# A graph attention layer in blocks: X W stored by chunks and gathered in two parts, weights read from PSUM, one row turned earlier

## The chip, the cores and the metric

The kernel runs on one core of a Trainium2 chip. TensorE (PE) multiplies matrices, with its weight loads shown as PEld; VectorE (DVE), ScalarE (ACT) and GpSimd (POOL) work on elements; SyncE (SP) and POOL issue DMAs, and 16 DMA engines carry them between HBM and the on-chip memories SBUF and PSUM. The metric is the device time of one execution in microseconds. One execution was also taken by the profiler; the times in the texts that have two decimals are from its trace, and L1133 is line 1133 of the kernel before.

## The reference

Four layers, each x = layernorm(x + f(x)), over a graph of N = 2708 nodes with 128 features. `adj` is a dense 2708 x 2708 float32 matrix with mostly zeros.

```python
# layer 0: k = 4 nearest neighbours by distance of z, added to the adjacency
z = leaky_relu(lap_mul(A, x) @ W1 + b1, 0.1)
S = exp(-sqrt(d2(z) + 1e-10) / 2), kept for the 4 nearest of each row
out = lap_mul(S + A, x) @ W2 + b2
# layer 1: attention
XW = X @ W
s_col, s_row = XW @ a[:128], XW @ a[128:]
den = exp(leaky_relu(s_row[:, None] + s_col[None, :], 0.01))
num = A @ den
att = where(num != 0, den / num, 0)
H = A @ (att @ XW)
# layer 2: h = d A d x;  h @ W.T + b
# layer 3: relu([x, A x] @ W.T + b)
```

## The kernel before

**Tiles.** The nodes stand in 22 row tiles of 128 (FULL = 21 whole ones, and a last one of 20 nodes) and, as columns of `adjT`, in C = 6 chunks: four of 512, one of 384, one of 276. A pass over the adjacency takes, for each chunk, four panels of four row tiles each by DMA from SP (L175, 1 MB for a chunk of 512) into the slots of `ring`, and six resident row tiles (`res`).

**Layer 1 by ranks.** The term leaky_relu(s_row + s_col) takes one of two slopes, by whether s_row is over −s_col. So den is e^r e^c on one side of a threshold and e^.01r e^.01c on the other. The kernel sorts the columns of den by c into 44 blocks of 62 (two columns more carry running sums from block to block), and keeps for each node r, e^r (`e_r`), e^.01r (`f_r`) and, as a row on all partitions, e^.99r (`gb`). The stages:

- *Pass 2* of layer 0 (until about 443 us). `by_panels` runs the product; after each panel a list of chores with due times (`Due`, `at`) puts in work on the finished chunk: near gathers (L669, indirect DMAs from POOL that fetch the nearest neighbours' rows; DVE's near sums add them up), `norm0` (the layernorm), `turn` (transposes), `find_c`, `compare` (a mask of every node's c against one row tile's, on DVE), `times_w` (PE's X W, copied by ACT into `xwe`, which holds X W and r), `rank_rows` and `rank_columns` (ACT and PE count ranks).
- *The thresholds' wait* (443 to 463). The last chunk's chores; then rr (r copied out of `xwe`), e_r and f_r (L861 to L863), the store of X W to HBM from POOL (L874, and L877 for the last 20 rows), and the thresholds: `pick_c`, `to_all` (a product with ones that puts a sum on all partitions), and `lc`, the 32 columns of weights of each row tile.
- *The rank stage* (463 to 541). PE sums the adjacency over coarse blocks: `part_sum` (L1133) multiplies 128 x 32 of `lc` by a row tile of a chunk. Four row tiles stand in four groups of 32 columns of one PSUM tile, beside one another. `end_sums(c)` (ACT L1142, PE L1144, ACT L1145) folds them into `carry`. After every panel, `between(c, i0)` puts a chore into the order, which is written out by hand (`manual_schedule`) for PE, DVE and ACT:
  - `find_blocks`: each node's block; `into_places(js, ...)` (PE L981): the columns put in sorted places, as one-hot matrices times values;
  - `ranked`: `row_j` and `csort` out of `js`, a memset of `xws` (POOL L1002) and 22 gathers of the rows of X W in sorted order (POOL L1005); `g_col` = e^.99c and `g_inv` = e^−.99c;
  - `count`, `find_values` (DVE L1047 to L1054), `find_places`: the place of each node in its block's list; `into_places(sl, ...)` and `listed` (L1100 to L1109): the list of rows of each block, with e and f of each;
  - `on_all` (PE L871, ACT L872): a column of values, turned by 128 x 128 transposes into PSUM, then copied through Exp into a row on all partitions: `g_row` of csort at (2,0) to (2,12), and `gb` of rr at (3,20) and (4,0);
  - `weights`: the weights of each block's list, 62 columns each, made from `g_row` by DVE for odd blocks (L1117) and ACT for even blocks (L1121), and a maximum with 0 on DVE (L1124) for each four odd ones.
- *The block loop* (541 to 773). 44 steps, 22 pairs of blocks for each half of the columns. `load(i)` gathers the listed rows of the adjacency (POOL L1264, two a step) and two rows of `carry` (SP). `find_num` (PE L1384), `invert` (ACT Ln and Exp), DVE's mix, and `add` (PE L1243, with a block's 128 rows of `xws`, which ACT scales in place by `g_col` in the step's own turn). `load(i + 2)` is issued in step i. A power on POOL in the first steps (L254) gives `dinv`.
- Layers 2 and 3 (773 to the end).

PSUM tiles of the rank stage: three for `part_sum`, three of the kind `mis` for everything that is turned or put on all partitions, one each for the places and the counts. A dense version of layer 1 stands behind a branch (`flag`) and isn't run here.

Of the kernel before, what the change touches and what calls it, by code (L numbers as in the profile page):

```python
# [8 lines left out]
F32 = mybir.dt.float32  # L9
# [7 lines left out]
P = 128  # L17
# [35 lines left out]
def kernel(  # L53
# [96 lines left out]
    hT = big.tile([P, N], F32, tag="hT", name="hT")  # L150
# [99 lines left out]
    def inv_sqrt_of(dst, src, eps):  # L250

        if in_arm:
            nc.vector.tensor_scalar_add(dst, src, eps)  # L253
            nc.gpsimd.tensor_tensor(dst, dst, minus_half[:, : dst.shape[-1]], op=ALU.pow)  # L254
        else:
            nc.vector.tensor_scalar_add(dst, src, eps)
            inv_sqrt(dst, dst)
# [10 lines left out]
    def normalize(ts, xs):  # L268
# [7 lines left out]
        inv_sqrt_of(rstd[:, : t1 - t0], mv[:, t0:t1, 1], LN_EPS)  # L276
# [437 lines left out]
    def norm0(ts):  # L714
# [11 lines left out]
        normalize(ts, xs)  # L726
# [24 lines left out]
    def times_w(c, t):  # L751
# [3 lines left out]
        nc.scalar.copy(xwe[:p, t, : D + 1], po[:p, : D + 1])  # L755

# [33 lines left out]

    due = Due()
# [8 lines left out]
    def end_pass2(c, acc):  # L800
# [9 lines left out]
        if c < C - 1:  # L810
# [3 lines left out]
            for k, t in enumerate(ts):  # L814
                at(n + 13 + 2 * k, compare, t)
                at(n + 14 + 2 * k, times_w, c, t)
                if c == C - 2 and k == len(ts) - 1:
# [5 lines left out]
        else:  # L823
            for t in behind_last:
                at(n + 1, rank_rows, t)
            at(n + 2, norm0, ts)
            at(n + 3, turn, c)
            at(n + 4, find_c, c)
            for k, t in enumerate(ts):
                at(n + 5 + k, compare, t)  # L830
                at(n + 5 + k, times_w, c, t)
                at(n + 5 + k, rank_rows, t)
                at(n + 6 + k, rank_columns, t)

# [18 lines left out]

    with tc.tile_pool(name="rank", bufs=1) as rank:
# [6 lines left out]
        nc.vector.tensor_copy(rr, xwe[:, :, D])  # L861
        nc.scalar.activation(e_r, rr, AF.Exp)
        nc.scalar.activation(f_r, rr, AF.Exp, scale=0.01)  # L863

        def on_all(row, col, n0=0, n1=NQ):

            for o in range(n0 * P, min(n1 * P, row.shape[-1]), CW):
                e = min(row.shape[-1], o + CW)
                ps = mis_tile()
                for k in range(o, e, P):  # L870
                    nc.tensor.transpose(ps[:, k - o : k - o + P], col[:, k // P : k // P + 1].to_broadcast([P, P]), ident)  # L871
                nc.scalar.activation(row[:, o:e], ps[:, : e - o], AF.Exp, scale=0.99)  # L872

        nc.gpsimd.dma_start(  # L874
            xw_rows[: FULL * P, :].rearrange("(t p) d -> p t d", p=P), xwe[:, :FULL, :D]
        )
        nc.gpsimd.dma_start(xw_rows[FULL * P :, :], xwe[:LAST, FULL, :D])  # L877
# [11 lines left out]
        def pick_c(ranks, name):  # L889

            n = ranks.shape[-1]
            first = big.tile([P, n, T], F32, tag="hT", name=name)
# [15 lines left out]
        c_head = to_all(pick_c(edge[:, 0:NB:CH], "head"))  # L908
# [85 lines left out]
        hot_in = big.tile([P, N], F32, tag="hT", name="hot_in")  # L994
        hot = [ones_at(b_j, n) for n in range(3)]

        def ranked(js):
# [5 lines left out]

            for q in range(NQ):
                nc.gpsimd.indirect_dma_start(  # L1005
                    out=xws[:, q, :], out_offset=None, in_=xw_rows[:, :],
                    in_offset=bass.IndirectOffsetOnAxis(ap=row_j[:, q : q + 1], axis=0), bounds_check=N - 1,
                    oob_is_err=False,
                )
# [7 lines left out]
        two_b = wide.tile([P, T, NB], BF16, tag="wide", name="two_b")  # L1017
# [94 lines left out]
        def weights(lw, g_row, blocks):  # L1112
            for s in blocks:
                for b in (s, s + 1):
                    w, g = lw[:, b, 2:], g_row[:, b * (BJ + 2) + 2 : (b + 1) * (BJ + 2)]
                    if b % 2:
                        nc.vector.tensor_scalar(  # L1117
                            w, g, slot_e[:, b : b + 1], slot_f[:, b : b + 1], op0=ALU.mult, op1=ALU.add
                        )
                    else:  # L1120
# [456 lines left out]
```

## Time and profile before

| | us |
|---|---|
| four runs | 1117.26, 1115.72, 1133.07, 1126.06 |
| their median | 1121.66 |
| the profiled execution | 1112.36 |
| its span in the trace | 1110.5 |

| stage of the span | us | PE busy | DVE busy | ACT busy | POOL busy |
|---|---|---|---|---|---|
| load and pass 1, 0 to 157 | 157.0 | 124.41 | 97.72 | 13.10 | 12.49 |
| nearest neighbours, 157 to 284 | 127.0 | 126.30 | 122.50 | 73.09 | 9.08 |
| pass 2, 284 to 443 | 159.0 | 135.96 | 89.91 | 42.77 | 79.33 |
| thresholds' wait, 443 to 463 | 20.0 | 7.60 | 14.72 | 10.25 | 2.10 |
| rank stage, 463 to 541.2 | 78.2 | 64.50 | 35.19 | 20.67 | 32.94 |
| block loop, 541.2 to 773 | 231.8 | 222.57 | 213.47 | 157.00 | 94.83 |
| layers 2 and 3, 773 to 1110 | 337.0 | 322.49 | 72.10 | 27.55 | 27.08 |

The busy times are sums over the stretch named. In the lists of the trace, a line such as "507.19 4.95 PE acc L1133 x35" gives a start, a length, the engine, the tile written, the line of the kernel and the number of instructions. "issue" is time in which the engine waited for nothing that the profile shows. "another core or an unknown queue" and "remote" stand where the event that released an instruction has no writer in the trace. PEclk is the clock that TensorE was granted, as a share of the full one.

### The profile page before, as it was taken

How to read it: one execution, taken by the hardware profiler on the slowest of the kernel's cores; microseconds unless marked ns; L12 is line 12 of the kernel's file. 1: busy time of each engine (PE TensorE's matmuls, PEld its weight loads, DVE VectorE, ACT ScalarE, POOL GpSimd, SP SyncE). 2: the span in 40 equal slices, each digit the busy share in tenths (PEclk: the TensorE clock that was granted, in tenths of full speed). 3: DMA queues.
4: the chain of work that ended last, by engine and by line, in shares of the span. 5: the costliest groups of instructions: out<-in, count | busy, mean ns of one | idle time of the engine just before them, and what ended most of it. 6: DMA issues, size and time to landing. Idle time of an engine off the chain costs nothing.

```text
span 1110.5 us, 11430 instructions
## 1 busy us (share of the span) xinstructions
PE 1003.8 (90%) x3678; PEld 482.9 (43%) x3678; DVE 645.6 (58%) x1366; ACT 344.4 (31%) x626; POOL 257.9 (23%) x325
## 2 busy tenths in 40 slices
PE   0899999999978889597789999999999999999996
PEld 0356544444434456243233333333444644465444
DVE  5984549999824467863379999998212112122122
ACT  0000135555301235323557676666001100011000
POOL 4000000001575442035454343441111200000000
PEclk9989999999998899598999999999999999999998
DMA  9998330000474445595544444446574865574752
GB/s 341 369 303 274 114 113 1 1 0 1 145 253 149 136 139 186 194 346 160 152 114 140 137 128 145 154 144 207 165 254 152 269 227 190 175 248 141 254 156 76
DMA packets 109283, 190.30 MB, mean 171 GB/s; under 512 B 13570, under 2 KB 46610, under 8 KB 109214
## 3 DMA queue, kind: packets, MB, share of 16 engines
q1 hardware_dynamic: 91582, 151.86, 41.3%
q0 software_dynamic: 17632, 37.62, 11.0%
q8 instruction: 31, 0.51, 0.2%
q14 instruction: 38, 0.31, 0.1%
HBM read 214.37 MB, written 4.16 MB: 197 GB/s over the span
## 4 chain that ended last, share of the span: by engine, by line
PE 75%; DMA 8%; DVE 6%; issue 4%; POOL 3%; ACT 2%; another core or an unknown queue 2%; SPq 1%; POOLq 0%; DVEq 0%; ACTq 0%
PE acc L201 31%; PE acc L639 9%; PE num L1384 8%; PE hacc L1243 7%; PE acc L424 7%; DMA res<-in_adjT 3%; PE acc L629 2%; PE acc L1133 2%; DMA ring<-carry 2%; DMA ring<-in_adjT,slot_i 2%; PE mis L286 1%; DVE both L479 1%; DVE mask L767 1%; POOL ring L125 1%
## 5 line engine op out<-in xcount | busy, mean ns | idle before, releaser
L1264 POOL DMA_INDIRECT ring<-in_adjT,slot_i x88 | 96.1, 1092 | 136.3 <-PE num L1384 110.0
L1384 PE MATMUL num<-ring,lw 128*64 128x512 f32 (+1 forms) x528 | 118.1, 560 | 9.4 <-DMA ring<-in_adjT,slot_i 3.7
L1243 PE MATMUL hacc<-inv,xws 128*128 128x512 f32 (+1 forms) x264 | 111.6, 559 | 0.3 <-ACT inv L1221 0.3
L639 PE MATMUL acc<-zT,z 128*128 128x512 f32 (+4 forms) x264 | 106.9, 551 | 0.0
L1218 ACT ACTIVATE inv<-num,plain 128x1024 f32<-128x1024 f32 x88 | 80.6, 916 | 69.5 <-PE num L1384 64.2
L1228 DVE TENSOR_TENSOR err<-inv,num 128x1024 f32<-128x1024 f32 x88 | 74.8, 855 | 35.6 <-ACT inv L1221 34.3
L254 POOL TENSOR_TENSOR rstd<-rstd,minus_half 128x4 f32<-128x4 f32 (+1 forms) x18 | 17.3, 961 | 313.5 <-DVE rstd L253 313.5
L640 ACT COPY key<-acc 128x512 f32<-128x512 f32 (+3 forms) x132 | 70.2, 535 | 58.1 <-issue 29.8
L235 ACT COPY gb<-acc 128x512 f32<-128x512 f32 (+2 forms) x18 | 9.6, 535 | 251.1 <-PE acc L201 251.1
L669 POOL DMA_INDIRECT got<-y_rows,where x66 | 70.2, 1064 | 57.7 <-DVE near_sum L682 31.5
L201 PE MATMUL acc<-ring,y 128*128 128x512 f32 (+2 forms) x192 | 82.0, 556 | 1.4 <-DMA ring<-in_adjT 0.8
L1243 PEld LDWEIGHTS hacc<-inv,xws 128*128 128x128 f32 x264 | 46.5, 189 | 77.6 <-issue 43.6
L201 PE MATMUL acc<-ring,xs 128*128 128x512 f32 (+2 forms) x192 | 77.8, 549 | 0.0
L1235 DVE SCALAR_TENSOR_TENSOR inv<-gb,g_inv,inv 128x1024 f32<-128x1024 f32 x88 | 77.0, 914 | 0.1
L201 PE MATMUL acc<-ring,carry 128*128 128x512 f32 (+2 forms) x192 | 74.5, 542 | 0.0
L201 PE MATMUL acc<-ring,m_rows 128*128 128x512 f32 (+2 forms) x192 | 74.3, 542 | 0.0
L1232 DVE SCALAR_TENSOR_TENSOR inv<-err,inv 128x1024 f32<-128x1024 f32 x88 | 72.6, 864 | 0.1
L639 PEld LDWEIGHTS acc<-zT,z 128*128 128x128 f32 (+1 forms) x264 | 46.9, 186 | 53.9 <-issue 48.5
L1384 PEld LDWEIGHTS num<-ring,lw 128*64 128x64 f32 x528 | 38.2, 138 | 70.9 <-issue 48.9
L1221 ACT ACTIVATE inv<-inv 128x1024 f32<-128x1024 f32 x88 | 67.6, 768 | 2.8
L641 DVE MAX8 near<-key 128x8 f32<-128x2708 f32 (+1 forms) x22 | 65.3, 2970 | 3.5 <-ACT key L640 3.5
L642 DVE FIND_INDEX8 where<-near,key 128x8 uint32<-128x2708 f32 (+1 forms) x22 | 65.4, 2972 | 0.0
(323 smaller groups left out, 1322.3 us busy)
## 6 DMA issues: line engine op xcount, KB each, us to landing
ring<-in_adjT SPq DMA_DIRECT2D x86, 1024.0 KB
ring<-in_adjT SPq DMA_DIRECT2D x19, 768.0 KB
part<-in_adjT SPq DMA_DIRECT2D x12, 1024.0 KB
ring<-in_adjT SPq DMA_DIRECT2D x19, 552.0 KB
res<-in_adjT SPq DMA_DIRECT2D x4, 1280.0 KB
more<-in_adjT SPq DMA_DIRECT2D x4, 1024.0 KB
part<-in_adjT SPq DMA_DIRECT2D x3, 768.0 KB
part<-in_adjT SPq DMA_DIRECT2D x3, 552.0 KB
```

The lines of the kernel that those rows point to most:

```text
L201: nc.tensor.matmul(accs[c][: lhsT.shape[-1], :w], lhsT=lhsT, rhs=src, start=start, stop=stop)
L424: nc.tensor.matmul(accs[c][:, : cw[c]], lhsT=y[:, i, :], rhs=src[:, : cw[c]], start=first, stop=last)
L639: nc.tensor.matmul(pks[c][:p, : cw[c]], lhsT=z2[:, :p], rhs=zT[:, cs], start=False, stop=True)
L640: nc.scalar.copy(key[:p, cs], pks[c][:p, : cw[c]])
L669: nc.gpsimd.indirect_dma_start(out=got[:p, :], out_offset=None, in_=y2_rows[:, :], in_offset=bass.IndirectOffsetOnAxis(ap=where[:p, t, k : ...
L1218: nc.scalar.activation(inv, num[:, :w], AF.Ln, scale=plain[:, 0:1], bias=plain[:, 1:2])
L1228: nc.vector.tensor_mul(err, inv, num[:, :w])
L1232: nc.vector.scalar_tensor_tensor(inv, err, 2.0, inv, op0=ALU.subtract, op1=ALU.mult)
L1235: nc.vector.scalar_tensor_tensor(inv, gb[:, col : col + w], g_inv[:, q : q + 1], inv, op0=ALU.max, op1=ALU.mult)
L1243: nc.tensor.matmul(haccs[:, o:e], lhsT=xws[:, q, :], rhs=inv[:, o:e], start=(q == 0), stop=(q == NQ - 1))
L1264: nc.gpsimd.indirect_dma_start(out=rows[i][:KC, n, :], out_offset=None, in_=adj_half[:, :], in_offset=bass.IndirectOffsetOnAxis(ap=slot_i[ ...
L1384: nc.tensor.matmul(num[n * (BJ + 2) : (n + 1) * (BJ + 2), o:e], lhsT=lw[:, 2 * q + n, :], rhs=rows[i][:, n, c0 + o : c0 + e], start=True, ...
```

## The change

- *X W is stored chunk by chunk.* `keep_xw(c)` is put behind the last `times_w` of each chunk, so that its DMA issues stand in POOL's queue among the near gathers of pass 2. For the last chunk the three `times_w` come before the compares.
- *The last chunk's layernorm* takes its inverse square root by a power on POOL instead of ACT's square root and DVE's reciprocal, and ACT's Exp table is loaded before that chunk's transposes are copied.
- *gb in the thresholds' wait.* rr is copied before the last compare, `exp_r` adds `gb_col` = e^.99r, and the 22 transposes with their six ACT copies stand around the product that puts the head's sum on all partitions: eight before it, 14 behind. The row goes where `xwe` stood, so it waits for the last store of X W.
- *Weights from PSUM.* `g_row` is gone. `g_col` is turned by fours into a PSUM tile, and DVE and ACT read that tile, eight blocks to a tile, with a maximum after each.
- *Row tile 20* of the six chunks is summed for three chunks at once, each in a group of its own, as the last row tile of 20 nodes was before.
- *The chores of the rank stage* are put in another order: `find_blocks` at (0,8) instead of (0,20), three of the four parts of `js` and `find_values` at (1,4), `count` at (2,0), the fourth part, `find_places` and `ranked` at (2,4), the parts of `sl` at (3,0) and (3,4), weights from (3,8) to (4,8).
- *The X W gathers:* 14 (SOON) in `ranked` as before, eight in steps 0 to 7 of the block loop, each behind `load(i + 2)` on POOL.
- `m_rows` and `two_b` move to other buffers.

```diff
+    def keep_xw(c):
+        ts = chunk_tiles[c]
+        t0, t1 = ts[0], min(ts[-1] + 1, FULL)
+        nc.gpsimd.dma_start(
+            xw_rows[t0 * P : t1 * P, :].rearrange("(t p) d -> p t d", p=P), xwe[:, t0:t1, :D]
+        )
+        if t1 <= ts[-1]:
+            nc.gpsimd.dma_start(xw_rows[FULL * P :, :], xwe[:LAST, FULL, :D])
...
+    def find_r():
+        nc.vector.tensor_copy(rr, xwe[:, :, D])
+
+    def exp_r():
+        nc.scalar.activation(e_r, rr, AF.Exp)
+        nc.scalar.activation(f_r, rr, AF.Exp, scale=0.01)
+        nc.scalar.activation(gb_col, rr, AF.Exp, scale=0.99)
...
             for k, t in enumerate(ts):
                 at(n + 13 + 2 * k, compare, t)
                 at(n + 14 + 2 * k, times_w, c, t)
+                if k == len(ts) - 1:
+                    at(n + 14 + 2 * k, keep_xw, c)
...
-            at(n + 2, norm0, ts)
+            at(n + 1, exp_table)
+            at(n + 2, norm0, ts, True)
             at(n + 3, turn, c)
             at(n + 4, find_c, c)
+            for t in ts:
+                at(n + 4, times_w, c, t)
+            at(n + 4, keep_xw, c)
             for k, t in enumerate(ts):
+                if k == len(ts) - 1:
+                    at(n + 5 + k, find_r)
                 at(n + 5 + k, compare, t)
-                at(n + 5 + k, times_w, c, t)
...
-        nc.gpsimd.dma_start(
-            xw_rows[: FULL * P, :].rearrange("(t p) d -> p t d", p=P), xwe[:, :FULL, :D]
-        )
-        nc.gpsimd.dma_start(xw_rows[FULL * P :, :], xwe[:LAST, FULL, :D])
...
+        def turned(col, n0):
+
+            ps = mis_tile()
+            for k in range(n0, min(n0 + 4, NQ)):
+                nc.tensor.transpose(ps[:, (k - n0) * P : (k - n0 + 1) * P], col[:, k : k + 1].to_broadcast([P, P]), ident)
+            return ps
...
+            for n in range(n0, n1, 4):
+                ps, e = turned(col, n), min(row.shape[-1] - n * P, CW)
+                nc.scalar.copy(row[:, n * P : n * P + e], ps[:, :e])
...
-        c_head = to_all(pick_c(edge[:, 0:NB:CH], "head"))
+        head = pick_c(edge[:, 0:NB:CH], "head")
+        gb = wide.tile([P, T * D], F32, tag="wide", name="gb")[:, :N]
+        on_all(gb, gb_col, 0, 8)
+        c_head = to_all(head)
+        on_all(gb, gb_col, 8, T)
...
-            for q in range(NQ):
-                nc.gpsimd.indirect_dma_start(
...
+            for q in range(SOON):
+                fetch_xw(xws, q)
...
+        def weights(lw, n0):
+
+            g_all = turned(g_col, n0)
+            n1 = min(n0 + 4, NQ)
+            for b in range(2 * n0, 2 * n1):
+                o = (b - 2 * n0) * (BJ + 2) + 2
+                w, g = lw[:, b, 2:], g_all[:, o : o + BJ]
+                if b % 2:
+                    nc.vector.tensor_scalar(
+                        w, g, slot_e[:, b : b + 1], slot_f[:, b : b + 1], op0=ALU.mult, op1=ALU.add
+                    )
+                else:
+                    nc.scalar.activation(w, g, AF.Relu, scale=slot_e[:, b : b + 1], bias=slot_f[:, b : b + 1])
+            half = lw[:, 2 * n0 + 1 : 2 * n1 : 2, 2:]
+            nc.vector.tensor_scalar_max(half, half, 0.0)
...
-            if (c, i0) == (0, 20):
...
+            if (c, i0) == (0, 8):
+                c_edge = to_all(c_part)
+                find_blocks(c_edge)
...
+            if (c, i0) == (1, 4):
+                for n in range(3):
+                    into_places(work["js"], hot[n], val_q[:, :, :2, :], n)
                 hot.append(ones_at(b_j, 3))
+                find_values()
             if (c, i0) == (2, 0):
+                work["counts"] = count()
+            if (c, i0) == (2, 4):
                 into_places(work["js"], hot[3], val_q[:, :, :2, :], 3)
+                find_places(*work["counts"])
                 work["xws"] = ranked(work["js"])
...
+            if (c, i0) == (3, 0):
                 work["sl"] = js_pool.tile([P, CW], F32, tag="places", name="sl")
+                for n in range(3):
+                    into_places(work["sl"], hot[n], val_b, n)
                 hot.append(ones_at(pos, 3))
+            if (c, i0) == (3, 4):
                 into_places(work["sl"], hot[3], val_b, 3)
                 work["lw"] = listed(work["sl"])
...
+            if (c, i0) in ((3, 8), (3, 12), (3, 16), (4, 0), (4, 4), (4, 8)):
+                weights(work["lw"], 4 * work["groups"])
+                work["groups"] += 1
...
+                if i0 + 4 >= FULL - 1 and begins:
+                    for n in range(c, c + GROUPS):
+                        part_sum(n, FULL - 1, n - c, res[:, FULL - 1 - S, cols[n]])
...
+                late_q = list(range(SOON, NQ))
                 find_num(0, "wide")
                 find_inv(0, "wide")
                 for i, (h, q) in enumerate(steps):
                     if i + 2 < len(steps):
                         load(i + 2)
+                    if late_q:
+                        fetch_xw(xws, late_q.pop(0))
```

## The prediction

> **What bounds the kernel now.** I read the page's shares and its chain of waits first. TensorE carries three quarters of what ends last:
>
> ```profile
> PE 1003.8 (90%) x3678; PEld 482.9 (43%) x3678; DVE 645.6 (58%) x1366; ACT 344.4 (31%) x626; POOL 257.9 (23%) x325
> ...
> PE 75%; DMA 8%; DVE 6%; issue 4%; POOL 3%; ACT 2%; another core or an unknown queue 2%; SPq 1%; POOLq 0%; DVEq 0%; ACTq 0%
> ```
>
> So an edit pays only where PE stands idle. The change works between 355 and 590 us; busy time by stretches of the rank stage (columns: window; length; busy and instructions of PE, PEld, DVE, ACT, POOL; clock; DMA share; GB/s):
>
> ```profile
> 473.80:487.60 13.80, 13.80 (x99) 7.13 (x100) 5.36 (x11) 2.15 (x4) 0.00 (x0) 1.00 1.05 387
> 487.60:499.80 12.20, 10.89 (x86) 4.89 (x85) 11.67 (x21) 3.59 (x8) 10.20 (x7) 1.00 0.84 290
> 499.80:511.05 11.25, 11.25 (x89) 6.88 (x88) 1.61 (x7) 1.17 (x2) 8.68 (x9) 1.00 0.57 185
> 511.05:523.00 11.95, 4.94 (x12) 1.20 (x11) 6.56 (x29) 7.36 (x22) 7.81 (x8) 0.72 0.37 113
> 523.00:541.23 18.23, 13.95 (x109) 6.30 (x110) 0.33 (x2) 5.74 (x12) 6.26 (x6) 0.87 0.63 183
> ```
>
> PE is full until 511 and then loses 7.0 of 11.95 us, and 4.3 of the next 18.2. DMA is at 0.37 there, so panels aren't short. The chain of waits over that stretch (start, length, what):
>
> ```profile
> 507.19 4.95 PE acc L1133 x35
> ...
> 512.79 0.83 issue
> ...
> 516.20 1.72 issue
> ...
> 519.71 1.75 issue
> ...
> 522.91 2.18 PE mis L871 x9
> ...
> 533.39 3.37 another core or an unknown queue
> ...
> 537.26 2.03 another core or an unknown queue
> ...
> 541.23 3.14 PE num L1384 x8
> ```
>
> PE waits on nothing that is shown; single instructions come late. What else runs then, from the timelines of POOL, VectorE and ScalarE:
>
> ```profile
> 487.63 2.45 POOL L1002 MEMSET xws<- 128x2816 f32 x1 [29.00 <-PE js L981]
> 490.36 1.09 POOL L1005 DMA_INDIRECT xws<-xw_rows,row_j  x1 [0.28 <-DVE plain L1050]
> ...
> 519.99 1.00 POOL L1005 DMA_INDIRECT xws<-xw_rows,row_j  x1 [0.30 <-issue]
> 510.06 0.31 DVE L1100 TENSOR_SCALAR slot_i<-sl 128x44 uint32<-128x44 f32 x2 [8.40 <-PE acc L1133]
> 521.48 0.29 DVE L1124 TENSOR_SCALAR lw<-lw 128x248 f32<-128x248 f32 x1 [3.07 <-remote]
> 511.05 7.36 ACT L1121 ACTIVATE lw<-g_row,slot_f,slot_e 128x62 f32<-128x62 f32 x22 [3.24 <-issue]
> ```
>
> The 22 gathers of X W leave POOL every 1.31 us from 490.36 on. The list's matmuls (L981) end at 507.19, and DVE reads them at 510.06, 2.87 late; DVE then waits 3.07 for its own result. All this ends 2 us after the last gather. I read it as signals that arrive late under a long run of indirect DMAs; pass 2 shows it too (11.11 in the chain at 330.33, in a run of near gathers begun at 307; 6.21 at 357.88), and the burst of 372 to 388 has none. The lag began 10 to 21 us into a burst.
>
> The Trainium skill ("SBUF — State Buffer", "Who interferes with whom") lets only VectorE and GpSimd contend for a port, and TensorE and ScalarE never. The memset row agrees (VectorE's 2.11 us f_out beside its 2.45), the late PE row doesn't fit; by that rule shortening the burst would return nothing to PE.
>
> **The change, part by part** (on the clock of before's profile)
>
> *Pass 2.* Seven issues of the X W store stand among the near gathers, 0.60 to 1.50 us each (L877, L874). By the ends of the xwe copies (365.3, 394.0, 410.1, 431.8, 442.7, 450.4) and the bursts (372.2–387.8, 395.1–410.9, 416.8–424.3), most fall where POOL is idle; the second adds 0.6, the third holds tile 19's gathers from 408.3 to about 411.4, and those have some 6 us in hand. Zero; if not covered, up to 3. Behind a store that waits stand near gathers, and behind those DVE's near sums; the last store stands behind the power. Power on POOL costs 0.85 to 1.04 (L254) in place of 0.21 on ScalarE and 0.18 on DVE, on the way to the last chunk's xs, and rr's copy adds 0.18 before the last compare: **+0.6**. The table load (1.28, L862) moves into ScalarE's idle time of 446: zero, as DVE set the pace of the wait it leaves; 1.3 if it delays xT's copy.
>
> *Thresholds' wait.* 22 transposes (0.27 to 0.47) and six copies (0.60) of gb go where PE is busy 1.29 of 5.45 us, but three PSUM tiles and a clock of 0.50 make PE end them at about 464.6; part sums begin there, not at 462.95: **+1.6**, that +0.6 included. ScalarE's first gb copy also waits for the last X W store, whose buffer it takes; the old store's packets ran from 457 to 462.5 for 21 tiles, the last of the new ones has two and a bit, issued near 452: zero, or up to 5 us for PE, c_head and all of DVE's cuts behind it if that landing is late. Where gb's transposes stood (L871, 519.3 to 528.7) PE gets back 4.5, and row tile 20 summed for three chunks at once makes two passes of about 0.59 out of six of 0.4 to 0.6: about 2 more.
>
> *The list.* Between js (487.6) and the counts (493.72) DVE did 5.9 us of values (L1047 to L1054, memset's contention included); they now come while PE is at part sums. The list stands at 511.05 − 5.9 − 2.87 + 1.6 = **503.9**.
>
> *Weights.* Six copies of g_row (0.60) go. But both engines read one PSUM tile and each instruction waits for the other's: ScalarE 0.42 + VectorE 0.31 + two hand-offs of 0.04 is 0.81 a pair, 22 pairs **18 us**, where the 7.36 row of ScalarE ran beside VectorE. The bounds are 7.4 (no alternation) and 18; I take 18, as the built order has the waits. Behind a weight that waits are queued DVE's maxima, ScalarE's copies of end_sums and, on PE, the next transposes with all sums behind them, since there are three such PSUM tiles and end_sums needs one: 503.9 + 18 = 521.9, with two end_sums among them (2.2) 524.1, then the last three panels and two end_sums (5.3): the block loop starts at **529.4** if no signal is late, not at 541.23: **−11.8**. By TensorE's sum, 464.6 + 64.6 busy − 4.5 − 2 + 1.1 and 1.3 idle + 2.6 tail = 527.7, so weights bind by little.
>
> The skill's "PSUM — Partial Sum Buffer", "PSUM bank collisions raise a hardware error", says that two engines may not be at one bank together, reads included; it would make the alternation unavoidable and speaks against this change. No row of before has such a pair.
>
> *Late signals.* Fourteen gathers run from 494.1 to 512.4. With a lag from an age of 10 to 21 us, it covers 0 to 8 us of the weights, at 0.59 lost per us (7.0 of 11.95): 0 to 4.7; I take 2. The ring's gathers before the loop stay (3.37 + 2.03): 0 to 5.4; I take half, 2.7, as bursts with and without lag stand side by side. Start **534.1**, −7.1.
>
> *The loop.* Eight X W gathers join two ring gathers of 1.05 + 0.30 in steps of 4.9 us: 4.05 of 4.9, it fits; the product that reads a gathered row stands 14 steps later, so its landing costs nothing. The dinv power shows already what a POOL hold does:
>
> ```profile
> 558.18 2.92 POOL dinv L254
> ...
> 565.17 9.60 DMA ring<-in_adjT,slot_i
> ```
>
> It cost PE one wait of 3.14 us (574.82); a gather or two ahead of it adds 0 to 2.7. I take **+1.5**. Lags are the second rival.
>
> Sum: −7.1 + 1.5 = −5.6. The profiled execution took 1112.36 (span 1110.5), 9.3 below the median of the runs; I give the same difference to the median: 1121.66 − 5.6 = **1116**.
>
> **Rivals.** (1) No late signal any more: −11.8, and 0 to −3 more if the loop's wait goes: 1107 to 1110. For it: 14 gathers are a burst shorter than the 22 whose lag was seen from an age of 20 us; against it: near bursts lagged from 10. (2) Slower: eight loop steps keep POOL issuing at 83% of a burst's rate for 39 us, and signals between PE, ScalarE and VectorE run late there, where each step is a chain of hand-offs. With lag from 10 us on, 29 us × 0.59 = 17, net +10 or 1132; from the start 23, net +16 or 1138; it passes 1% once the lag begins within 8 us. Against: at two gathers per step, before's loop lags are at most 1.9 us. (3) The list is earlier, but each of the 44 alternations takes a lag of 0.15 us (6.6 us) and the ring's 5.4 stay: 529.4 + 12.0 = 541.4, with the loop's 1.5 1123. (4) The change doesn't do what it says: near gathers wait behind stores and pass 2 grows by 3 to 6, giving 1119 to 1122.
>
> **How the numbers follow.** About 1% (11 us) is what can be told from no change here, as the four runs spread over 17. Forecast (1112 to 1120) 0.38, rival 1 0.27, rival 2 0.18, rivals 3 and 4 0.17. Faster by over 1% (below 1110.4): rival 1 and a little of the forecast, 0.32. Slower (above 1132.9): rival 2 and a little, 0.20. Same 0.48. The range goes from 1104 (rival 1 with the loop's wait gone, and 1.7 more if weights run side by side and TensorE's 527.7 binds: 1105, less 1 for the rows' own spread) to 1132 (rival 2's milder end).
>
> **What would show it.** slot_e's writes (L1106 before) at about 504; ScalarE's and VectorE's weights in turn, 0.8 us a pair, 22 pairs; no single late PE instructions between 511 and 523; first num at 529 to 537; steps 0 to 7 at 4.9 us, with three gathers each. Wrong if the loop's first eight steps take more than 45 us, if weights run side by side, or if pass 2 ends over 2 us later.

## The result and the profile after

| | before | after |
|---|---|---|
| median of the runs, us | 1119.65 (69 runs) | 1121.47 (43 runs) |
| ratio to before, with its 95% interval | | 1.0018 (1.0004 to 1.0032) |
| profiled execution, us | 1112.36 | 1120.05 |
| its span | 1110.5 | 1118.3 |

The forecast was 1116, faster by 5.6 us; the measured change is a loss of 1.8 us, with 0.4 to 3.6 by the interval. The page of after, its busy shares and its chain of waits:

```profile
PE 1009.6 (90%) x3678; PEld 483.8 (43%) x3678; DVE 646.3 (58%) x1365; ACT 342.1 (31%) x620; POOL 265.4 (24%) x331
...
PE 60%; issue 17%; POOL 9%; DMA 7%; DVE 4%; ACT 2%; SPq 1%; POOLq 0%; another core or an unknown queue 0%; DVEq 0%; ACTq 0%
```

POOL stands in the chain with 9% where it had 3%, "issue" with 17% where it had 4%. A second trace of the same kernel (after_again, below) has 3% and 4% again, so these shares belong to one execution and nothing is read from them. The stretches of the rank stage, with the columns and the windows shown of before:

```profile
473.80:487.60 13.80, 13.71 (x92) 6.38 (x93) 8.94 (x20) 1.85 (x5) 0.00 (x0) 0.88 0.91 326
487.60:499.80 12.20, 12.20 (x104) 7.07 (x103) 6.53 (x13) 2.05 (x5) 6.10 (x4) 1.00 1.05 386
499.80:511.05 11.25, 10.44 (x77) 4.57 (x76) 2.95 (x11) 1.61 (x4) 8.59 (x9) 1.00 0.87 280
511.05:523.00 11.95, 5.14 (x9) 0.99 (x10) 3.22 (x10) 3.58 (x9) 2.45 (x3) 0.55 0.39 112
523.00:541.23 18.23, 12.75 (x90) 4.70 (x90) 4.41 (x14) 6.37 (x16) 7.33 (x7) 0.78 0.39 105
```

The hole is where it was: from 511 to 523 PE is busy 5.14 of 11.95 us (4.94 before). The timeline of ScalarE there:

```profile
508.87 0.40 ACT L1163 ACTIVATE lw<-mis,slot_f,slot_e 128x62 f32<-128x62 f32 x1 [0.41 <-issue]
509.68 0.40 ACT L1163 ACTIVATE lw<-mis,slot_f,slot_e 128x62 f32<-128x62 f32 x1 [0.41 <-issue]
515.80 0.40 ACT L1163 ACTIVATE lw<-mis,slot_f,slot_e 128x62 f32<-128x62 f32 x1 [5.71 <-remote]
516.61 0.40 ACT L1163 ACTIVATE lw<-mis,slot_f,slot_e 128x62 f32<-128x62 f32 x1 [0.41 <-DVE lw L1159]
```

The weights start 4 us earlier than before and go 0.81 us a pair, as worked out. Then ScalarE stands idle for 5.71 us where it waited 0.41 from pair to pair. (A hand-off is one engine's instruction waiting for another engine's.) This one came over 5 us late. POOL's last up-front gather, from its timeline:

```profile
513.11 1.00 POOL L890 DMA_INDIRECT xws<-xw_rows,row_j  x1 [0.30 <-issue]
```

It ends at 514.1, 1.7 us before ScalarE goes on. Two other stretches differ. Pass 1, which the change doesn't touch, waits longer for its last chunk; PE's row of before, then of after:

```profile
90.12 2.13 PE L424 MATMUL acc<-part,y 128*128 128x276 f32 x8 [1.27 <-DMA part<-in_adjT]
```

```profile
93.01 3.53 PE L427 MATMUL acc<-part,y 128*128 128x276 f32 x8 [3.52 <-DMA part<-in_adjT]
```

And in the block loop PE waits longer for rows of carry and for gathered rows (us in all, times, longest; 3.3 and 3.7 in all before):

```profile
PE num L1420 <- DMA ring<-carry: 5.8, 6, 1.6
PE num L1420 <- DMA ring<-in_adjT,slot_i: 5.3, 6, 1.8
```

### The profile page after: what moved, and what is told of

Read it like the earlier page. It is cut to its first block, busy times and chain, and to the rows that moved or that the text cites. A ratio compares the mean times of both kernels' runs of the same rounds, so it can differ in the third digit from the quotient of the medians.

```text
span 1118.3 us, 11444 instructions
## 1 busy us (share of the span) xinstructions
PE 1009.6 (90%) x3678; PEld 483.8 (43%) x3678; DVE 646.3 (58%) x1365; ACT 342.1 (31%) x620; POOL 265.4 (24%) x331
## 4 chain that ended last, share of the span: by engine, by line
PE 60%; issue 17%; POOL 9%; DMA 7%; DVE 4%; ACT 2%; SPq 1%; POOLq 0%; another core or an unknown queue 0%; DVEq 0%; ACTq 0%
PE acc L204 34%; PE acc L642 8%; PE acc L427 7%; POOL ring L1298 5%; DMA res<-in_adjT 3%; DMA ring<-in_adjT,slot_i 2%; PE acc L632 2%; POOL xws L890 1%; PE num L1420 1%; PE hacc L1277 1%; PE mis L289 1%; DMA part<-in_adjT 1%; DMA ring<-in_adjT 1%; ACT junk L792 1%; DVE both L482 1%
## 5 line engine op out<-in xcount | busy, mean ns | idle before, releaser
L1420 PE MATMUL num<-ring,lw 128*64 128x512 f32 (+1 forms) x528 | 121.7, 557 | 13.6 <-DMA ring<-carry 5.8
L643 ACT COPY key<-acc 128x512 f32<-128x512 f32 (+3 forms) x132 | 70.1, 534 | 58.2 <-issue 29.8
L204 PE MATMUL acc<-ring,y 128*128 128x512 f32 (+2 forms) x192 | 80.6, 548 | 1.3 <-DMA ring<-in_adjT 0.8
L645 DVE FIND_INDEX8 where<-near,key 128x8 uint32<-128x2708 f32 (+1 forms) x22 | 65.4, 2972 | 0.0
```

The costliest lines, as they stand in the source:

```text
L204: nc.tensor.matmul(accs[c][: lhsT.shape[-1], :w], lhsT=lhsT, rhs=src, start=start, stop=stop)
L643: nc.scalar.copy(key[:p, cs], pks[c][:p, : cw[c]])
L1420: nc.tensor.matmul(num[n * (BJ + 2) : (n + 1) * (BJ + 2), o:e], lhsT=lw[:, 2 * q + n, :], rhs=rows[i][:, n, c0 + o : c0 + e], start=True, ...
```

## The experiments

Each run left one trace. The table reads the same marks off each, in us: "near" is the last copy of the nearest neighbours' keys, from the span's start; "list" goes from the first part sum to the list's last write (L1109 before); "weights" from there to the last weight; "rank" from the first part sum to the first num; "ten steps" from VectorE's mix of step 0 to that of step 10. Most steps take 4.9 (the median of every trace), so ten steps without a wait are 49.

| kernel | near | list | weights | rank | ten steps | ratio to before (95%) |
|---|---|---|---|---|---|---|
| before | 288.6 | 48.2 | 12.0 | 78.3 | 55.9 | |
| before_again | 289.6 | 45.4 | 7.5 | 78.7 | 55.6 | one execution |
| after | 292.9 | 40.4 | 28.2 | 76.1 | 57.8 | 1.0018 (1.0004 to 1.0032) |
| after_again | 293.8 | 38.8 | 28.3 | 74.4 | 61.7 | one execution |
| changed_third | 295.0 | 43.7 | 26.5 | 77.8 | 58.8 | 1.0018 (0.9982 to 1.0054) |
| changed_pad | 295.1 | 38.8 | 25.1 | 71.2 | 58.2 | 1.0043 (1.0020 to 1.0066) |
| spread_2 | 294.4 | 38.5 | 20.6 | 65.8 | 59.8 | 0.9975 (0.9935 to 1.0014) |
| no_gather | 293.9 | 38.5 | 20.1 | 65.4 | 52.6 | 0.9943 (0.9912 to 0.9975) |
| plain_dma | 293.7 | 43.5 | 20.6 | 72.4 | 57.0 | one execution |
| by_tile | 294.1 | 43.7 | 21.5 | 75.9 | 57.5 | 0.9978 (0.9946 to 1.0009) |
| combo | 295.3 | 43.5 | 15.5 | 70.5 | 53.5 | 0.9916 (0.9877 to 0.9955) |
| before_spread | 290.3 | 45.4 | 7.2 | 69.5 | 57.8 | 0.9945 (0.9910 to 0.9980) |
| before_best | 289.1 | 47.0 | 7.2 | 71.1 | 52.6 | 0.9913 (0.9877 to 0.9949) |
| before_store | 290.3 | 54.3 | 7.4 | 80.6 | 55.8 | 0.9988 (0.9953 to 1.0023) |
| old_store | 294.3 | 40.4 | 25.0 | 73.1 | 55.6 | 1.0037 (1.0001 to 1.0073) |
| before_row, other chip | 289.5 | 47.0 | 7.3 | 69.1 | 58.0 | 0.9993 (0.9962 to 1.0025) |
| all_up_front, other chip | 296.4 | 38.8 | 20.2 | 65.1 | 63.8 | 1.0078 (1.0049 to 1.0108) |
| early_power, other chip | 296.6 | 40.4 | 20.2 | 66.6 | 54.3 | 0.9997 (0.9966 to 1.0029) |
| held_third, other chip | 295.0 | 40.2 | 13.9 | 59.3 | 54.3 | 1.0036 (1.0009 to 1.0063) |

The four marked "other chip" ran on a chip where the kernel before took 1094.08; on the others it took 1114 to 1120. Theory A is that signals come late under a run of indirect DMAs; B, that the alternating weights decide; C, that the third gather of a step costs the loop.

Two cautions. The traced execution need not be the median one: those of combo (1116.31) and all_up_front (1110.63) are the slowest of their runs, that of changed_pad (1109.52) the fastest. And the column "list" goes with the clock that TensorE was granted. In the changed kernels it is 38.5 to 38.8 where the clock up to the list was 0.98 or 0.99, 40.2 to 40.4 at 0.92 to 0.96, and 43.5 to 43.7 at 0.88 (changed_third, plain_dma, by_tile, combo). The stretch from the first part sum to the list in spread_2, then in plain_dma (the clock is the third number from the end):

```profile
466.54:505.07 38.53, 36.98 (x286) 18.16 (x286) 25.37 (x60) 4.78 (x13) 4.73 (x3) 0.98 0.96 342
```

```profile
462.73:506.20 43.47, 41.32 (x286) 19.19 (x286) 25.36 (x60) 4.77 (x13) 8.81 (x13) 0.88 0.90 312
```

Sixteen part sums on PE in spread_2, and the same sixteen in plain_dma:

```profile
483.23 1.92 PE L1173 MATMUL acc<-ring,lc 128*32 128x512 f32 x16
```

```profile
481.71 3.64 PE L1173 MATMUL acc<-ring,lc 128*32 128x512 f32 x16
```

These part sums end before the first DMA of X W's rows into `xws` (495.8 and 497.0), so that run can't have slowed them. What lowered the clock isn't shown. So a difference between two of these rank stages is read without the part that stands in the list.

### The run of gathers

*after_again* and *changed_third* are the changed kernel, unedited.

> The changed kernel once more, for a second trace. Theory A (signals arrive late under the 14 up-front gathers of X W) expects the stall again at the same place: between about 508 and 516 ScalarE's weights stand still some 4 to 7 us, until about 2 us after POOL's last up-front gather; the block loop starts at 538 to 542. If the stall were an accident of one execution, the weights would run through at 0.81 us a pair and the loop would start at about 530.

> The changed kernel itself, timed against the kernel before on one chip. Theory A: where the chip shows late signals the rank stage is 74 to 77 (from the first part sum to the loop's start) and the ratio 0.998 to 1.006; where it shows none, the rank stage is 64 to 67, the ratio 0.994 to 1.002, because pass 1's 4 us and the loop's 2 to 6 take back most of the gain. If the rank stage is 74 to 77 without late signals, theory A falls.

The stall came back in both, 4.34 us in after_again and 4.25 in changed_third, so it was no accident of one execution. It came back, shorter, in two kernels of the section on pass 1 too, whose rank stage is that of the changed kernel: 3.58 in changed_pad and 2.90 in old_store. In these two it ended while POOL was still at its 14 gathers. ScalarE and POOL in changed_pad, each from its timeline:

```profile
510.18 0.40 ACT L1163 ACTIVATE lw<-mis,slot_f,slot_e 128x62 f32<-128x62 f32 x1 [3.58 <-remote]
```

```profile
511.13 1.00 POOL L890 DMA_INDIRECT xws<-xw_rows,row_j  x1 [0.31 <-issue]
```

So the end of the run isn't what ends the stall in every execution; what does isn't shown.

*spread_2*: two gathers up front, 20 in the loop.

```diff
-    SOON = 14
+    SOON = 2
```

> Two X W gathers up front, 20 in the block loop, one a step. Theory A: no long run of gathers in the rank stage, so no stall of ScalarE or PE between 508 and 516; the list stands at 503 to 505, weights take 18 us, block loop starts at 529 to 533, some 8 to 11 before the changed kernel's 540.74. Theory C (three gathers a step cost the loop): loop of 20 such steps grows by another 5 to 12 over the changed kernel's 241.8, so that the whole is 1112 to 1126. Theory B alone (the alternating weights decide, gathers don't matter): start stays at 537 to 541.

*no_gather*: the 22 gathers left out, so that layer 1 has nothing of X W.

```diff
-            for q in range(SOON):
-                fetch_xw(xws, q)
...
-                late_q = list(range(SOON, NQ))
+                late_q = []
```

> Leaves out the 22 gathers of X W altogether (xws stays zero), so layer 1 adds nothing. Theory A and C together: the start of the block loop is as with two up front, 529 to 533, and the loop is no longer than in the kernel before (234) or 1 to 4 shorter; in all 8 to 18 us below the changed kernel. Theory B alone: start at 537 to 541 and only the loop is shorter. This is the most that any order of the gathers can give.

Both lost the stall, and started the loop at 532.38 and 530.97. ScalarE in spread_2, at the time of the hole:

```profile
512.37 0.40 ACT L1163 ACTIVATE lw<-mis,slot_f,slot_e 128x62 f32<-128x62 f32 x1 [0.69 <-DVE lw L1159]
513.18 0.40 ACT L1163 ACTIVATE lw<-mis,slot_f,slot_e 128x62 f32<-128x62 f32 x1 [0.41 <-DVE lw L1159]
513.99 0.40 ACT L1163 ACTIVATE lw<-mis,slot_f,slot_e 128x62 f32<-128x62 f32 x1 [0.41 <-DVE lw L1159]
514.29 0.58 ACT L1182 COPY tot<-acc 128x512 f32<-128x512 f32 x1
```

B alone falls: the weights alternate as in the changed kernel, and the stage is 8.6 us shorter than in after_again, on the same chip with the same list. Against the kernel before the whole gained only 0.25% in spread_2, which its interval doesn't tell from nothing: the loop took 244.2 where it had taken 233.9 and 239.4, and pass 1 some 4 more.

*plain_dma*: 14 plain DMAs from POOL instead, so X W stands there in its stored order.

```diff
-                fetch_xw(xws, q)
+                nc.gpsimd.dma_start(xws[:, q, :], xw_rows[q * P : (q + 1) * P, :])
```

> The 14 up-front gathers are replaced by 14 plain DMAs from POOL of as many rows of X W in their stored order, so X W stands in the wrong order there. Theory A in the form that indirect DMAs make signals late: no stall, loop's start as with two gathers up front (66 us after the first part sum). In the form that any run of DMAs that POOL issues, or their packets, makes them late: a stall as in the changed kernel, until 2 us after the last of the 14, and 74 to 76 us.

POOL and ScalarE, each from its timeline:

```profile
496.96 4.25 POOL L1049 DMA_DIRECT2D xws<-xw_rows  x8 [0.29 <-POOL xws L1047]
```

```profile
510.48 0.40 ACT L1163 ACTIVATE lw<-mis,slot_f,slot_e 128x62 f32<-128x62 f32 x1 [0.69 <-DVE lw L1159]
...
533.46 0.39 ACT L1182 COPY tot<-acc 128x276 f32<-128x276 f32 x1 [5.46 <-remote]
```

A plain DMA takes POOL 0.53 us, a gather 1.0 and 0.3 of pause; no stall in the weights (20.6). The stage was 72.4 and not 66 for two reasons: 4.9 us lie before the list, under the lower clock, and 1.6 behind the weights, where ScalarE's last copy waited 5.46 (3.83 in spread_2), until 0.9 us after the last of the ring's six gathers and one of X W, which stay. But the plain DMAs also ended at 508, so how long POOL issues and what it issues aren't told apart here.

### Weights by tile

*by_tile*: one engine for each PSUM tile of weights.

```diff
-                if b % 2:
+                if n0 // 4 % 2:
                     nc.vector.tensor_scalar(
...
-            half = lw[:, 2 * n0 + 1 : 2 * n1 : 2, 2:]
-            nc.vector.tensor_scalar_max(half, half, 0.0)
+            if n0 // 4 % 2:
+                half = lw[:, 2 * n0 : 2 * n1, 2:]
+                nc.vector.tensor_scalar_max(half, half, 0.0)
```

> Each PSUM tile of turned g_col is read by one engine: ScalarE takes groups 0, 2, 4 of eight blocks, VectorE groups 1, 3, 5. Theory B: no more alternation, ScalarE 0.33 a block and VectorE 0.24, the weights take about 9 us rather than 18, and the loop starts 5 to 9 us earlier than 540.74. Theory A: the first groups are still held until 2 us after the 14 gathers (about 516), the rest then runs fast: start 4 to 6 earlier. If PE's sums and the tail bind instead, less than 3.

Two rows from the timelines, ScalarE's first tile and VectorE's:

```profile
509.96 2.46 ACT L1163 ACTIVATE lw<-mis,slot_f,slot_e 128x62 f32<-128x62 f32 x8 [9.47 <-PE mis L908]
```

```profile
517.84 2.09 DVE L1159 TENSOR_SCALAR lw<-mis,slot_e,slot_f 128x62 f32<-128x62 f32 x8 [10.20 <-remote]
```

POOL's last up-front gather:

```profile
515.81 1.01 POOL L890 DMA_INDIRECT xws<-xw_rows,row_j  x1 [0.30 <-issue]
```

Eight blocks take 2.46 or 2.09 where four alternating pairs took 3.2. VectorE's tile was turned at 509.4, and VectorE began at 517.84, 1.0 after the last gather's end. So the weights gained 6.8 us against after_again and not more: A, not B. The loop's start gained nothing (539.78 against 539.99), which neither theory had forecast: 4.9 us went before the list, under the lower clock, and 3.3 behind the weights.

### Parts of the change on the kernel before, and the loop

*before_again* is the kernel before. *before_spread* has its gathers spread as in spread_2, and nothing else.

> The kernel before once more, for a second trace, to see which stages of its first one were of that execution alone. The first trace had the nearest neighbours' end at 288.6 (292.9 to 294.4 in all five traces of changed kernels, whose code there is the same) and a loop of 233.9. If those were luck of one execution, the second trace has the end nearer 293 and the loop at 236 to 241; the rank stage's stall between 511 and 523 should be there in both, ending about 2 us after the last of 22 gathers, and the loop's start 76 to 79 us after the first part sum.

> The kernel before with one part alone: two X W gathers up front and 20 in the block loop, all else as it was. Theory A: the stall of 511 to 523 goes, the rank stage takes 66 to 70 us from the first part sum to the loop's start instead of 78.3, the loop pays 3 to 8; in all 2 to 8 faster than the kernel before. Theory B (the order of the chores decides): rank stage stays within 3 of 78.3 and the kernel gets slower by what the loop pays.

The second trace of before has the same rank stage and a loop of 239.4; the 233.9 of the first, and with it a good part of the 9.3 by which that execution lay below the median, was its own. before_spread is faster than before and after alike: rank 69.5. So with the run of gathers gone the whole rest of the change is worth about 69.5 − 65.8 = 3.7 us in this stage (two chips; on the one without the lag 69.1 in before_row against 66.6 and 65.1 in early_power and all_up_front). The loop cost what C said, 244.4 against 239.4.

The power that gives dinv is moved out of the loop next. *early_power* is the changed kernel with that power in the rank stage, *combo* has that, weights by tile and two gathers up front; *all_up_front* is the changed kernel with SOON = 22 and the power where it was.

```diff
+            if (c, i0) == (1, 8):
+                inv_sqrt_of(dinv, deg, DEG_EPS, True)
...
-        inv_sqrt_of(dinv, deg, DEG_EPS)
```

> Two gathers up front and 20 in the loop, one engine for each PSUM tile of weights, and the dinv power moved from the loop's start to the rank stage at (1,8), where POOL has nothing to do. Theory A with C: weights run without a stall and without alternation, the rank stage takes 58 to 63 us; without the power's 4 to 5 us on POOL the loop's steps 6 to 9 (6.3 to 7.8 in the changed kernel) are 4.9 to 5.5, the loop 230 to 236. In all 1104 to 1111, 9 to 16 below the kernel before. If the backlog came from the third gather and not from the power, the loop stays at 241 to 245 and the kernel at 1111 to 1116.

> The changed kernel with the dinv power (4 to 5 us on POOL) moved from the loop's start to the rank stage at (1,8). Theory C, that the power holds the loop's gathers up and the third gather only slows the recovery: steps 6 to 9 (7.8, 6.7, 7.8, 6.3 us in the changed kernel) become 4.9 to 6, the loop 234 to 239 instead of 241.8, the kernel 4 to 8 faster. If the third gathers themselves do it, steps 6 to 9 stay over 6. The power may hold VectorE by up to 4 us where both run, which moves the list later by as much.

> The changed kernel with all 22 X W gathers up front, none in the loop. Theory A: the run of gathers lasts from 495 to 524, the alternating weights stand still until about 526 except for what gets through before the lag, and the loop starts at 547 to 553 (rank stage 82 to 88 us). Theory C: the loop loses its third gathers and falls from 241.8 to 234 to 239. In all 3 to 9 slower than the changed kernel. If the lag hurt only as far as 14 gathers go, the start stays at 540 to 543 and the kernel gets faster by what the loop gains.

Without the power ten steps are 52.6 to 54.3, also with third gathers in some 20 steps (combo, held_third, before_best): third gathers alone are nearly hidden. The power alone is hidden in no_gather (52.6), but not in the kernel before: 55.6 to 55.9 in before, before_again and before_store, with one step of 9.0 to 10.5. With both it is 57.0 to 61.7 in all kernels but old_store (55.6). POOL falls behind: after the power it issues eleven gathers in after, and four in before, with pauses of no more than 0.3 us. The other chip has 58.0 and 63.8 with the power alone (before_row, all_up_front), so the price of each part isn't settled. In early_power two of the four steps forecast at 4.9 to 6 were 7.1 and 7.2.

combo gained 0.84%. Its loop, 241.7, missed the forecast of 230 to 236. Its rank stage missed the forecast by 8: the weights ran without a stall, but 4.9 us more than in spread_2 lie before the list, under the lower clock, and 4.9 more behind the weights, where ScalarE's last copy waited until 1.3 us after the seventh indirect DMA before the loop:

```profile
533.60 0.39 ACT L1183 COPY tot<-acc 128x276 f32<-128x276 f32 x1 [5.23 <-remote]
```

all_up_front was a miss that teaches more: on that chip 22 gathers, from 484.25 to 513.50, run beside the weights and cost them nothing (20.2), and before_row, which differs from the kernel before by one buffer's width, had no hole either. Why the first ten steps of all_up_front were slow, 63.8, stays open.

*held_third* is combo with three gathers up front and the next from step 1 of the loop on; POOL also waits for the first step's products before it gathers for the third.

```diff
-        rows[i] = strip(i).rearrange("p (n k) -> p n k", n=2)
+        at_slot = i if i < 2 else (0, 2, 1)[(i - 2) % 3]
+        rows[i] = strip(at_slot).rearrange("p (n k) -> p n k", n=2)
```

> The combination of two parts before (weights by tile, early power) with three gathers of X W up front, the next from step 1 of the loop on, and the third step's ring gathers in the slot of the first, so that POOL waits for the first step's products before it issues them. Theory A: before the loop POOL issues four ring gathers instead of seven indirect DMAs, done some 4 us earlier, and ScalarE's last two copies, which came 5.2 late in the combination, come at once: rank stage 64 to 67 us instead of 70.5, the kernel at 1101 to 1106, 3 to 5 below the combination. If the lag comes from any four indirect DMAs, the rank stage stays at 69 to 71.

The stage fell to 59.3, and PE then waited for the held rows, here in its timeline:

```profile
520.03 1.36 PE L1424 MATMUL num<-ring,lw 128*64 128x330 f32 x2 [4.67 <-DMA ring<-in_adjT,slot_i]
525.04 7.26 PE L1424 MATMUL num<-ring,lw 128*64 128x330 f32 x22 [3.65 <-DMA ring<-in_adjT,slot_i]
```

The kernel is slower than before. It ran on the chip without the lag, where holding the gathers had nothing to win, so the forecast for late signals wasn't tested.

*before_best*: before_spread with the power moved from the loop to (0,20), nothing else of the change.

```diff
                 work["js"] = js_pool.tile([P, CW], F32, tag="places", name="js")
+                inv_sqrt_of(dinv, deg, DEG_EPS, True)
```

> The kernel before with two gathers up front, 20 in the loop, and the dinv power at (0,20) of the rank stage, nothing else of the change. With theory A: rank stage 66 to 70, loop 235 to 243, no 4 us in pass 1; 6 to 14 faster than the kernel before where signals are late, 0 to 6 where they aren't. If the change's other parts are what made the combination fast (0.992), this one stays at 0.994 to 1.0.

It took 1103.84 against 1116.40 for the kernel before, 0.9913: faster than both kernels, and, each by its own chip, as fast as combo with none of the change's other parts.

### Pass 1

*before_row* widens hT's buffer in the kernel before; *before_store* has the stores by chunks there; *old_store* is the changed kernel with one store; *before_pad* and *changed_pad* add three and twelve products to the branch that isn't run.

```diff
-    hT = big.tile([P, N], F32, tag="hT", name="hT")
+    hT = big.tile([P, T * D], F32, tag="hT", name="hT")[:, :N]
```

> The kernel before with one part alone: the buffer of hT, hot_in and gb is 22 x 128 columns wide instead of 2708, as in the changed kernel, so that what lies behind it moves by 432 bytes a partition. In all traces of changed kernels pass 1 is 4 us later by its last chunk (nearest neighbours end at 292.5 to 295 instead of 288.6 to 290.3), although the instructions up to there are the same. If the moved buffers do it, the end is at 292 to 295 here and the kernel 3 to 5 slower than the kernel before; if not, 288 to 290.5 and the same time within 3.

> The kernel before with the store of X W by chunks alone. If the stores move whatever slows pass 1's small loads, the nearest neighbours end at 292.5 to 297 instead of 288.6 to 290.3 and the kernel is 2 to 4 slower; otherwise 288 to 291, and the kernel is within 2 of the kernel before: the stores in pass 2 are hidden, and the last store, which no longer carries all of X W, isn't waited for in the kernel before.

> The changed kernel with X W stored once behind the last chunk, as in the kernel before. The row gb takes the buffer of X W, so ScalarE's first copy of it waits for that store: part sums begin 3 to 6 later after the last compare. If the stores by chunks slow pass 1, the nearest neighbours end at 288 to 291 here; if not, at 292.5 to 297 and the kernel is 2 to 6 slower than the changed one.

> The kernel before with three products added in the dense branch, which isn't run, so that TensorE's code is 768 bytes longer (the changed kernel's is 320 longer). If the length or place of the code decides when pass 1's small loads land, the nearest neighbours end at 292.5 to 297 here, and the kernel is 3 to 5 slower; otherwise 288 to 290.5 and the same time within 3.

> The changed kernel with twelve products added in the branch that isn't run, 3072 bytes of TensorE's code. If the place of the code decides, the nearest neighbours end at another time than 292.9 to 296.6, perhaps at 288 to 290; otherwise they stay there, and the cause stays open.

None of them moved it: near was 289.5, 290.3, 294.3, 289.5 and 295.1. (before_pad's trace is of an execution of 1130.65 against a median of 1117.90, so only pass 1 is read from it.) The ratios of before_pad and changed_pad to before were 1.0034 (1.0003 to 1.0066) and 1.0043 (1.0020 to 1.0066). So three products that are never run made the kernel before 0.34% slower, where the whole change lost 0.18%. No run shows why, and a loss of this size can't be put down to what the change does alone. All traces agree on the place in pass 1: the last packet of the attention vector, 1024 bytes to each partition, ends 5.6 to 6.0 us after its issue in the kernel before and its variants, 7.6 to 8.9 in the changed ones, and the last chunk's panel queues behind it. Why is open.

## Why the prediction was wrong

**The bound and the hole: right.** PE's loss between 511 and 523 was read as signals late under a run of gathers. Three kernels take the run away, and the hole goes. Against a trace of the same chip the stage is shorter by 8.6 (spread_2), 9.0 (no_gather) and 9.2 us (before_spread). That it is signals that come late is read from rows such as VectorE's in by_tile, whose tile stood turned 8 us before; what delays them isn't shown.

**The list: right, in part by luck.** Predicted at 503.9, it stood at 504.95, and the first part sum at 464.57 against 464.6. But the nearest neighbours ended 4.3 us later than before, which no term had, and pass 2 with the thresholds' wait took 2.6 less where 1.6 more was forecast; the two cancel. From the first part sum to the list 39.3 was forecast, and the three traces of the changed kernel and that of changed_pad have 40.4, 38.8, 43.7 and 38.8, the long one under the lower clock.

**Weights: right.** 0.81 a pair was forecast and measured; list to last weight was to be 18 + 2.2 = 20.2 without late signals, against 20.1 in no_gather. Without them the stage was to take 529.4 − 464.6 = 64.8; it took 65.4 and 65.8.

The rule of the Trainium skill that no two engines may be at one PSUM bank together, within the same partition ("PSUM — Partial Sum Buffer", "PSUM bank collisions raise a hardware error") fits the rows: strict turns on one tile, and side by side on two tiles in combo. No run let two engines at one tile without turns.

**Late signals: the step that failed.** The sum put them at 2 for the weights and 2.7 at the end, so the stage at 534.1 − 464.6 = 69.5. It took 76.1, 6.6 more. The end was right (7.6 from the last weight to the first num where 5.3 was forecast without lag, so 2.3), and 1.1 lies before the list. The other 6.0 are the weights: 28.2 from list to last weight, 8.0 over the 20.2 and not 2. The other traces have 8.1 (after_again), 6.3 (changed_third) and 4.9 (changed_pad) there, all above the bound of 4.7. Bound and term came from a rate, 0.59 lost per us, read off PE's row of before, where much work stood queued without hand-offs. A chain of hand-offs doesn't go slower at that rate: one hand-off in it stands, for 3.6 to 5.7 us in these four traces, and from 510.5 to 515.8 in after not one weight was made. In before_again, where each engine had its 22 blocks to itself without hand-offs, the same run of gathers left the weights at 7.5. With that the gain of 11.8 shrinks to its part that isn't lag, 3.7 by before_spread against spread_2: the change had the hole in its old place, with another chain in it. On the chip without the lag there was no gain in the whole either: early_power is at 0.9997.

**The loop: mis-sized.** 1.5 was taken and 0 to 2.7 allowed; ten steps grew from 55.9 and 55.6 to 57.8, 61.7 and 58.8, by 2 to 6. The term weighed the third gather and the power one by one, not a backlog that both feed. Rival 2 asked for late signals there; the waits are for gathered rows and rows of carry, POOL's queue of gathers is behind, and the price stayed below the rival's. The whole loop varies as much: 233.9, 239.4 and 241.7 in before, before_again and before_store, 241.8 to 244.0 in the three traces of the changed kernel.

**Pass 1: not in the sum.** The end of the nearest neighbours is at 288.6 to 290.3 in seven traces of the kernel before and its variants, 292.9 to 296.6 in the others: some 4 us that no row of before could show. **Pass 2** with the thresholds' wait was put at +1.6; from near to the first part sum it went from 174.3 and 174.0 to 171.7, 171.8 and 166.4. Kernels with pass 2 as before have 168.9 to 172.1 as well (before_best, before_spread), so that gain isn't shown to be the change's. Together: +4 for pass 1, −2 to −8 for pass 2, −1 to −4 for the rank stage, +2 to +6 for the loop, about +2 in the medians.

**The rivals.** The third, start near 541 and 1123, is what happened in the end (540.74 and 1121.47), but its number came true by luck: by one long stand, not by 0.15 us on each hand-off. The reader of a single trace had one more trap: its loop was 5.5 shorter than that of the second trace.

## What to carry to other kernels

Where a chain of hand-offs between engines crosses a run of indirect DMAs, price one hand-off in it as standing (3 to 6 us here, on the chips that showed it), not the chain as slowed, and look for the run before reordering the chain: two gathers up front and the rest one a step, with a 4 us power moved out of POOL's busy stretch, gave 0.9913 (0.9877 to 0.9949), more than the 0.5% that the larger change was forecast to give. Price POOL's loads together, not one by one, and take two traces before the sum is made against one. Compare stages at the same granted clock.

## What the runs showed of the hardware

- The lag belongs to the chip, or to something that differs between chips: with the same 22 gathers at the same 1.3 us, the rank stage took 78.7 and 80.6 on two chips (before_again, before_store) and 69.1 on a third (before_row), and pass 2 with the thresholds' wait 168 to 174 against 154.5. On that chip the alternating weights of all_up_front took 20.2 under 22 gathers, as long as with none (20.1 in no_gather). The kernel before took 1094 there.
- The stall is of some us, and what ends it isn't shown. It ended 1.7 and 1.8 us after POOL's last up-front gather in after and after_again (515.80 after 514.1, 515.26 after 513.5), 1.0 after it in by_tile (517.84 after 516.8), at its end in changed_third (514.33 after 514.3), and before it in changed_pad (510.18, gathers until 512.1) and old_store (512.96, until 515.7). ScalarE's last copy before the loop came 0.9 and 1.3 us after the last indirect DMA in plain_dma and combo (533.46 after 532.6, 533.60 after 532.3).
- The late rows stand on ScalarE (5.71 in after, reading PSUM), on VectorE (3.07 in before, reading SBUF) and on PE (1.72 and 1.75 in before). By the Trainium skill ("SBUF — State Buffer", "Who interferes with whom") PE and ScalarE never wait for another engine's port, so ports don't explain their rows; read so, a shorter run of gathers would give them nothing, and the runs gave 8.6 to 9.2 us.
- With the same instructions, the list came 5 us later where TensorE's granted clock was lower: 38.5 us after the first part sum at 0.98 (spread_2), 43.5 at 0.88 (plain_dma, combo).
- The power of 128 x 22 elements took POOL 5.04 in the loop before, 4.02 in the loop after and 3.87 to 3.89 in the rank stage.
